# A graph transformer on one core: layer 1's attention adds its weighted values by accumulating DMAs issued from GpSimd

## The chip, the core and the metric

The kernel runs on one core of a Trainium2 chip. The core has a matrix engine (TensorE, PE in the profile), three engines for elementwise work (VectorE, DVE; ScalarE, ACT; GpSimd, POOL), an engine that only issues transfers (SyncE, SP), an on-chip memory (SBUF) of 128 partitions, a smaller accumulation memory (PSUM), and 16 DMA engines that move data between SBUF and the device's memory. Each engine takes its instructions in order from a queue of its own and waits on semaphores for the others. DMAs that GpSimd issues sit in GpSimd's queue and then in one DMA queue (q0 in the profile); SyncE and ScalarE issue into queues of their own.

The metric is the device time of one execution in microseconds.

## What is computed

Two layers of a graph transformer on 2708 tokens of width 512, with 8 heads of 64 and a feed-forward width of 2048, all in float32. The adjacency matrix has about nine neighbours in a row, and attention is masked to them:

```python
mask = adj.astype(jnp.float32) + jnp.eye(n)
q = (h @ Wq.T + bq).reshape(n, 8, 64)      # k and v alike
scores = jnp.einsum('nhd,mhd->hnm', q, k) / 8.0
scores = jnp.where(mask[None] == 0, -1e9, scores)
attn = jax.nn.softmax(scores, axis=-1)
ctx = jnp.einsum('hnm,mhd->nhd', attn, v).reshape(n, 512)
h1 = _layer_norm(h + ctx @ Wo.T + bo, ln1_g, ln1_b)
ff = relu(h1 @ W1.T + b1) @ W2.T + b2
h2 = _layer_norm(h1 + ff, ln2_g, ln2_b)    # the next layer's h
```

## The kernel before

**Lists in place of the mask.** Early in the run the kernel makes, for each token, a list of its neighbours, and sorts the tokens by the length of the lists into 22 tiles of up to 128 tokens. `CAPS` holds the longest list of each tile, from 22 entries in tile 0 to 3 in tile 21 (which has 20 tokens). Attention of a tile is then a loop over list entries: for entry s, GpSimd gathers for each of the 128 tokens one row of 1024 numbers, the key and the value of its s-th neighbour, from `kv_d` (L1113, an indirect DMA of 512 KB).

**Chunks.** The entries of a tile are taken two at a time (`SLOTS`); such a chunk is a tile `kv` of 128 x 2 x 1024 numbers. There are 111 chunks in a layer. A chunk goes through these steps:

- `weights` (L1148): VectorE multiplies the keys by the query (L1150) and sums over each head (L1156) into `sc`.
- `weigh` (L1163): ScalarE takes exponentials (L1169, into `p`). Then the values are multiplied by them, the second entry by eight ScalarE instructions (L1176), the first by one of VectorE (L1182). The first chunk of a tile writes its products straight into the accumulator `acc` (128 x 2 x 512); every later chunk writes them over its own values in `kv`, and one VectorE instruction adds those to `acc` (L1189). There are 89 such adds in a layer.
- `sums` (L1193), after a tile's last chunk: VectorE folds the two halves of `acc` together (L1197) and takes the sum of the exponentials and its reciprocal (`su`, L1209 and L1212).
- `divided` (L1215): ScalarE scales `acc` by the reciprocals into `cx` (L1220), which is what the rest of the layer asks for.

**The order by hand.** The schedule is manual: what stands earlier in the program stands earlier in its engine's queue. `attend` (L1759) is a generator that puts down one step at a time. In step k it first takes the next chunk from `loads`, which issues the gathers of chunk k + 3, then puts down `weights` of chunk k, `weigh` of chunk k - 1, `sums` if chunk k - 2 was the last of its tile, and `divided` if chunk k - 3 was. At the end, and after the second tile, empty steps let the last chunks through. In layer 1 a chunk has one of seven places in SBUF (five of the `kv` tag and two of weights that are no longer needed), so the gathers of chunk k + 3 overwrite chunk k - 4.

**Beside the feed-forward.** The tokens go through the rest of a layer in blocks of two tiles (`blocks`, L1754). `feed_forward` (L1475) runs over 16 slices f of the hidden width: eight matmuls into `pf` (L1523), the relu on ScalarE (L1534), and the second product of an earlier slice into `a` (L1496). After each slice the main loop (L1943) calls `advance`, which puts down as many steps of attention as the entry of `PACES` for that f allows; no more than three finished `cx` are held. At f = 10 and f = 11 it calls `until` for the two tiles of the next block, which puts down steps until their `cx` exist, and then `attended` (L1434) puts down their transposes (L1293), the output projection (L620, `o`) and the first layer norm. Before the last two products of a block `turned` puts down the transposes of the normed rows, and the block ends with the second norm and an indirect store of the result (L1076, `out`). Each `norm` (L1265) asks GpSimd for one small instruction, `rd` (L1275), and VectorE then waits for it (L1281). So GpSimd's queue in layer 1 holds gathers, `rd` and stores, in program order.

Layer 0 works alike, but with fewer `kv` places, and with a feed-forward of seven products instead of eight that takes more of VectorE.

Of the kernel before, what the change touches and what calls it, by code (L numbers as in the profile page):

```python
# [13 lines left out]
ALU = mybir.AluOpType  # L14
# [5 lines left out]
DM = 512  # L20
# [16 lines left out]
CAPS = (22, 14, 13, 12, 12, 11, 11, 10, 10, 9, 9, 9, 9, 8, 8, 8, 7, 7, 7, 6, 5, 3)  # L37
# [446 lines left out]
def by_edges(ctx: ExitStack, tc: tile.TileContext, x, xT, adj, layers, out, redo):  # L484
# [9 lines left out]
    nc = tc.nc  # L494
# [3 lines left out]
    NL = len(layers)  # L498
# [149 lines left out]
    def size(g):  # L648
        return min(P, N - g * P)
# [483 lines left out]
    def chunks_of(g):  # L1133
        S = CAPS[g]
        k = (S + SLOTS - 1) // SLOTS
        cuts = [-(-S * i // k) for i in range(k + 1)]
        return [(g, a, b - a) for a, b in zip(cuts, cuts[1:])]

    class Tile:


        def __init__(self, g, q):
            self.g, self.r, self.q = g, size(g), q
            self.sc = at.tile([P, LIST, NH], F32, tag="sc", name="sc", bufs=2)
            self.p = at.tile([P, LIST, NH], F32, tag="p", name="p", bufs=2)
            self.acc = None
# [16 lines left out]
        def weigh(self, kv, s0, c):  # L1163
            r, g, p = self.r, self.g, self.p
            if s0 == 0:
                self.acc = at.tile([P, SLOTS, DM], F32, tag="acc", name="acc", bufs=2)
                self.wide = c
            for s in range(s0, s0 + c):
                nc.scalar.activation(  # L1169
                    p[:r, s, :], self.sc[:r, s, :], AF.Exp, bias=minus[:r, g, s : s + 1]  # L1170
                )
            to = self.acc[:r] if s0 == 0 else kv[:r, :, DM:]
            for i in range(1, c):
                for h in range(NH):
                    hd = slice(h * DK, (h + 1) * DK)
                    nc.scalar.activation(  # L1176
                        to[:, i, hd],
                        kv[:r, i, DM + h * DK : DM + (h + 1) * DK],
                        AF.Copy,
                        scale=p[:r, s0 + i, h : h + 1],  # L1180
                    )
            nc.vector.tensor_tensor(  # L1182
                to[:, 0, :].rearrange("p (h d) -> p h d", d=DK),
                kv[:r, 0, DM:].rearrange("p (h d) -> p h d", d=DK),
                p[:r, s0, :].unsqueeze(2).to_broadcast([r, NH, DK]),
                ALU.mult,
            )
            if s0:
                nc.vector.tensor_tensor(  # L1189
                    self.acc[:r, :c, :], self.acc[:r, :c, :], kv[:r, :c, DM:], ALU.add  # L1190
                )

        def sums(self, peak):  # L1193
            r, g, S, acc, wide = self.r, self.g, CAPS[self.g], self.acc, self.wide
            while wide > 1:
                h = wide // 2
                nc.vector.tensor_tensor(  # L1197
                    acc[:r, :h, :], acc[:r, :h, :], acc[:r, wide - h : wide, :], ALU.add
                )
                wide -= h  # L1200
            nc.vector.tensor_reduce(
                peak[:r, g : g + 1],
                self.sc[:r, :S, :].rearrange("p s h -> p (s h)"),
                AX.X,
                ALU.max,
                apply_absolute_value=True,
            )
            su = small.tile([P, NH], F32, tag="su", name="su")
            nc.vector.tensor_reduce(  # L1209
                su[:r], self.p[:r, :S, :].rearrange("p s h -> p h s"), AX.X, ALU.add  # L1210
            )
            nc.vector.reciprocal(su[:r], su[:r])  # L1212
            self.su = su
# [26 lines left out]
    def loads(n):  # L1240

        ready = []
        for g, s0, c in (chunk for g in order for chunk in chunks_of(g)):
            r = size(g)
            kv = rows_of_keys(n)
            for s in range(s0, s0 + c):
                load = gather(kv[:r, s - s0, :], kv_d[n], idx[:r, g, s : s + 1])
                for move in written[n]:
                    tc.add_manual_dep(
                        load.ins,  # L1250
                        move.ins.name,
                        mybir.DependencyInfo(
                            mybir.DependencyClass.Sync, mybir.DependencyReason.DATA
                        ),
                        reason="every row of keys is in its place",
                    )
                written[n].clear()
            ready.append(kv)
            if len(ready) > EARLY:
                yield ready.pop(0)  # L1260
        yield from ready
# [497 lines left out]
    def attend(n, got):  # L1759

        peak = small.tile([P, NT], F32, tag="peak", name="peak", bufs=1)
        nc.vector.memset(peak, 0.0)
        loaded = loads(n)
        steps = []
        for g in order:
            cuts = chunks_of(g)
            steps += [(g, s0, c, i, i + 1 == len(cuts)) for i, (_, s0, c) in enumerate(cuts)]
            if g == order[1]:
                steps += [None] * 3
        steps += [None] * 3  # L1770
        kv = next(loaded)
        yield 0.0
        q, later = asked(n, order[0]), None
        done = [None] * 3
        for k, step in enumerate(steps):
            if step:
                g, s0, c, i, last = step
                if i == 0:
                    while q is None:
                        q = asked(n, g)  # L1780
                        if q is None:
                            yield None
                    t, q = Tile(g, q), None
                if k > 0:
                    kv = next(loaded)
                t.weights(kv, s0, c)
                if q is None and g != order[-1]:
                    q, later = later or asked(n, order[order.index(g) + 1]), None
                if g == order[-3] and i == 2:
                    later = asked(n, order[-1])  # L1790
                done.append((t, kv, s0, c, last))
            else:
                done.append(None)
            t3, t2, t1 = done[-4:-1]
            if t1:
                t1[0].weigh(*t1[1:4])
            if t2 and t2[-1]:
                t2[0].sums(peak)
            if t3 and t3[-1]:
                got[t3[0].g] = t3[0].divided()  # L1800
            yield c / SLOTS if step else 0.2
        nc.vector.tensor_reduce(flags[:, 4 + n : 5 + n], peak, AX.X, ALU.max)
        nc.vector.tensor_scalar(
            flags[:, 4 + n : 5 + n], flags[:, 4 + n : 5 + n], SAFE, None, ALU.is_le
        )
# [31 lines left out]
    got = {}  # L1837
# [42 lines left out]
    for n in range(NL):  # L1880
        last = n == NL - 1
        nxt = None if last else Layer(n + 1, layers[n + 1])
        if n > 0:
            streamed = now.queries(order[10:16])
            got = {}
# [196 lines left out]
```

## Time and profile before

| | |
|---|---|
| median of 2 runs | 1828.03 us (1827.94 to 1828.11) |
| the profiled execution, span from first to last instruction | 1827.1 us |
| outside the span (1828.03 - 1827.1) | 0.9 us |
| instructions | 22528 |
| mean granted TensorE clock | 0.999 |
| moved by DMA | 393.80 MB, 216 GB/s on average |
| gathers of keys and values, L1113, both layers | 420, of 1248 ns on GpSimd each |
| adds into `acc`, L1189, both layers | 178, of 1154 ns on VectorE each |
| layer 1's first block ends and its steady part begins | about 1184 us |
| layer 1's last `cx` | 1752 us |

The profiled execution's span plus 0.9 us is the median of the timed runs, so sums made on the trace can be set against the median directly. A page of the profile gives each engine's busy time as a share of the span. In a line of a group stand the source line, the engine, the operation, what is written and read, the count, then the busy time in us and the mean of one in ns, and last the idle time of that engine just before these instructions with what ended it. Busy time of an engine that others do not wait for costs nothing; what counts is which wait ends last in each stage.

### The profile page before, as it was taken

How to read it: one execution, taken by the hardware profiler on the slowest of the kernel's cores; microseconds unless marked ns; L12 is line 12 of the kernel's file. 1: busy time of each engine (PE TensorE's matmuls, PEld its weight loads, DVE VectorE, ACT ScalarE, POOL GpSimd, SP SyncE). 2: the span in 40 equal slices, each digit the busy share in tenths (PEclk: the TensorE clock that was granted, in tenths of full speed). 3: DMA queues.
4: the chain of work that ended last, by engine and by line, in shares of the span. 5: the costliest groups of instructions: out<-in, count | busy, mean ns of one | idle time of the engine just before them, and what ended most of it. 6: DMA issues, size and time to landing. Idle time of an engine off the chain costs nothing.

```text
span 1827.1 us, 22528 instructions
## 1 busy us (share of the span) xinstructions
PE 1807.5 (99%) x6563; PEld 1162.6 (64%) x6563; DVE 1457.5 (80%) x2447; ACT 949.1 (52%) x3271; POOL 798.9 (44%) x745
## 2 busy tenths in 40 slices
PE   9999999999999999999999999999999999999998
PEld 4444456666777867778677644666666666666666
DVE  5887778988989889898895257887898888889853
ACT  5771435645556545564543213665665565567531
POOL 3334755534455544454430042353464555456302
PEclk9999999999999999999999999999999999999999
DMA  9997987757576676765652876745564664555300
GB/s 340 369 335 256 371 283 245 236 169 241 195 255 228 197 236 196 219 233 181 228 191 70 287 257 248 285 160 180 178 228 150 228 224 169 195 197 194 133 14 21
DMA packets 158061, 393.80 MB, mean 216 GB/s; under 512 B 17514, under 2 KB 60894, under 8 KB 157928
## 3 DMA queue, kind: packets, MB, share of 16 engines
q0 software_dynamic: 70608, 252.12, 40.2%
q1 hardware_dynamic: 77162, 118.55, 18.7%
q10 hardware_dynamic: 10158, 21.61, 3.1%
q8 instruction: 53, 0.87, 0.2%
q14 instruction: 80, 0.66, 0.1%
HBM read 338.78 MB, written 53.44 MB: 215 GB/s over the span
## 4 chain that ended last, share of the span: by engine, by line
PE 89%; DVE 5%; issue 2%; ACT 2%; DMA 1%; POOL 1%; POOLq 0%; SPq 0%; DVEq 0%
PE pf L1523 18%; PE a L1496 17%; PE pf L1653 9%; PE k L620 8%; PE v L620 8%; PE q L620 8%; PE o L620 8%; PE c L1643 4%; PE a L1643 3%; PE tp L1293 2%; DVE sc L1156 1%; DVE kv L1150 1%; DMA forms<-form_d 1%; PE a L1677 1%; PE a L1673 1%
## 5 line engine op out<-in xcount | busy, mean ns | idle before, releaser
L1113 POOL DMA_INDIRECT kv<-kv_d,listed x420 | 524.0, 1248 | 291.2 <-DVE acc L1189 133.9
L1523 PE MATMUL pf<-hT,w 128*128 128x256 f32 (+1 forms) x1792 | 393.2, 367 | 0.1
L1523 PEld LDWEIGHTS pf<-hT,w 128*128 128x128 f32 x1792 | 323.5, 190 | 103.1 <-issue 64.4
L1496 PE MATMUL a<-w,ft 128*128 128x512 f32 x800 | 373.1, 592 | 0.0
L1176 ACT ACTIVATE kv<-kv,p 128x64 f32<-128x64 f32 x1232 | 311.0, 335 | 5.0
L1275 POOL TENSOR_TENSOR rd<-va,mhalf 128x1 f32<-128x1 f32 (+1 forms) x88 | 80.5, 914 | 520.6 <-DVE va L1273 520.5
L1150 DVE TENSOR_TENSOR kv<-kv,q 128x1024 f32<-128x1024 f32 (+1 forms) x222 | 256.9, 1157 | 13.3 <-DMA q<-q_d,ident_i 10.9
L1156 DVE TENSOR_REDUCE sc<-kv 128x16 f32<-128x1024 f32 (+1 forms) x222 | 257.9, 1162 | 7.6
L1189 DVE TENSOR_TENSOR acc<-acc,kv 128x1024 f32<-128x1024 f32 (+2 forms) x178 | 205.4, 1154 | 37.6 <-ACT kv L1176 23.0
L1653 PE MATMUL pf<-hT,w 128*128 128x256 f32 x1024 | 233.1, 379 | 1.6 <-ACT ft L1664 1.6
L1496 PEld LDWEIGHTS a<-w,ft 128*128 128x128 f32 x800 | 150.1, 190 | 113.2 <-issue 101.3
L1653 PEld LDWEIGHTS pf<-hT,w 128*128 128x128 f32 x1024 | 193.9, 190 | 35.4 <-issue 7.9
L1534 ACT ACTIVATE ft<-pf,b 128x256 f32<-128x256 f32 (+1 forms) x208 | 95.0, 459 | 197.6 <-PE pf L1523 195.2
L1169 ACT ACTIVATE p<-sc,listed 128x8 f32<-128x8 f32 x420 | 104.0, 296 | 147.2 <-DVE sc L1156 135.7
L620 PE MATMUL o<-wo,cT 128*128 128x512 f32 x336 | 151.0, 593 | 1.0 <-ACT cT L1298 1.0
L1664 ACT ACTIVATE ft<-pf,b 128x256 f32<-128x256 f32 x96 | 44.9, 468 | 160.5 <-PE pf L1653 160.5
L1182 DVE TENSOR_TENSOR kv<-kv,p 128x512 f32<-128x512 f32 (+1 forms) x178 | 123.4, 693 | 4.5 <-ACT p L1169 4.3
L620 PEld LDWEIGHTS o<-wo,cT 128*128 128x128 f32 x336 | 63.4, 190 | 74.7 <-issue 65.5
L745 DVE MAX8 tops<-code 128x8 f32<-128x247 f32 (+2 forms) x242 | 78.6, 400 | 28.3 <-ACT code L740 28.3
L1281 DVE SCALAR_TENSOR_TENSOR h<-h,rd,ln_b 128x512 f32<-128x512 f32 (+1 forms) x88 | 65.9, 749 | 39.5 <-POOL rd L1275 39.5
L1220 ACT ACTIVATE cx<-acc,su 128x64 f32<-128x64 f32 (+1 forms) x352 | 88.2, 333 | 12.9 <-DVE su L1212 7.4
L1455 DVE TENSOR_TENSOR h<-o,xb 128x512 f32<-128x512 f32 (+1 forms) x44 | 30.3, 688 | 80.0 <-PE o L620 65.0
(232 smaller groups left out, 2323.5 us busy)
## 6 DMA issues: line engine op xcount, KB each, us to landing
aj<-in_adj SPq DMA_DIRECT2D x42, 677.0 KB, 6.3
forms<-form_d SPq DMA_DIRECT2D x168, 128.0 KB, 4.2
kv_d<-kvs ACTq DMA_DIRECT2D x21, 512.0 KB, 5.5
xg<-in_xT SPq DMA_DIRECT2D x19, 512.0 KB, 7.4
w<-in_W SPq DMA_DIRECT2D x16, 512.0 KB, 6.2
kv<-kv_d,listed POOLq DMA_INDIRECT x420, 6.3
zT_d<-zT SPq DMA_DIRECT2D x22, 256.0 KB, 5.1
xb_d<-h SPq DMA_DIRECT2D x21, 256.0 KB, 5.7
```

Of the source, the lines that this page charges most:

```text
L620: nc.tensor.matmul(o[:r], xs(c), wm[:, c, :], start=(c == 0), stop=(c == NC - 1))
L1113: return nc.gpsimd.indirect_dma_start(out=to, out_offset=None, in_=table[:, :], in_offset=bass.IndirectOffsetOnAxis(ap=s, axis=0), bounds_ ...
L1150: nc.vector.tensor_tensor(kv[:r, :c, :DM], kv[:r, :c, :DM], self.q[:r].unsqueeze(1).to_broadcast([r, c, DM]), ALU.mult,)
L1156: nc.vector.tensor_reduce(self.sc[:r, s0 : s0 + c, :], kv[:r, :c, :DM].rearrange("p s (h d) -> p s h d", d=DK), AX.X, ALU.add,)
L1169: nc.scalar.activation(p[:r, s, :], self.sc[:r, s, :], AF.Exp, bias=minus[:r, g, s : s + 1])
L1176: nc.scalar.activation(to[:, i, hd], kv[:r, i, DM + h * DK : DM + (h + 1) * DK], AF.Copy, scale=p[:r, s0 + i, h : h + 1],)
L1182: nc.vector.tensor_tensor(to[:, 0, :].rearrange("p (h d) -> p h d", d=DK), kv[:r, 0, DM:].rearrange("p (h d) -> p h d", d=DK), p[:r, s0, : ...
L1189: nc.vector.tensor_tensor(self.acc[:r, :c, :], self.acc[:r, :c, :], kv[:r, :c, DM:], ALU.add)
L1496: nc.tensor.matmul(a[:r, cols], fts[f][:, c0 : c0 + r], self.w2[f // 2][:, f % 2, cols], start=(f == 0), stop=(f == NFC - 1),)
L1523: nc.tensor.matmul(pf[:, :w], self.w1[f // 2][:, c, f % 2 * P : f % 2 * P + P], hT[:, c, :w], start=(c == 0), stop=(c == NC - 1),)
L1643: nc.tensor.matmul(to, left, right, start=start, stop=stop)
L1653: nc.tensor.matmul(pf[:, :W], self.w1[j][:, c, f % 2 * P : f % 2 * P + P], hT[:, c, :], start=(c == 0), stop=(c == NC - 1),)
```

## The change

In layer 1 only (`by_dma`), the add of a later chunk leaves VectorE. A new method `added` issues it as a DMA from GpSimd whose source is the products in `kv` and whose destination is `acc`, with the operation add. It is put down one step later than the products, after the gathers of that step. The fold leaves `sums` and becomes a method of its own, `folded`; in layer 1 it is put down one step after `sums`, and `divided` one step after the fold, so that a tile's `cx` comes four steps after its last chunk and not three. One more empty step stands after the second tile and at the end. Layer 0 keeps its order.

```diff
-        def __init__(self, g, q):
+        def __init__(self, n, g, q):
             self.g, self.r, self.q = g, size(g), q
+            self.by_dma = n == NL - 1
...
-            if s0:
+            if s0 and not self.by_dma:
                 nc.vector.tensor_tensor(
                     self.acc[:r, :c, :], self.acc[:r, :c, :], kv[:r, :c, DM:], ALU.add
                 )
 
-        def sums(self, peak):
-            r, g, S, acc, wide = self.r, self.g, CAPS[self.g], self.acc, self.wide
+        def added(self, kv, s0, c):
+            r = self.r
+            if s0 and self.by_dma:
+                nc.gpsimd.dma_start(
+                    out=self.acc[:r, :c, :], in_=kv[:r, :c, DM:], accum_op=ALU.add
+                )
+
+        def folded(self):
+            r, acc, wide = self.r, self.acc, self.wide
             while wide > 1:
                 h = wide // 2
                 nc.vector.tensor_tensor(
                     acc[:r, :h, :], acc[:r, :h, :], acc[:r, wide - h : wide, :], ALU.add
                 )
                 wide -= h
+
+        def sums(self, peak):
+            r, g, S = self.r, self.g, CAPS[self.g]
...
-                steps += [None] * 3
-        steps += [None] * 3
+                steps += [None] * (3 + (n == NL - 1))
+        late = n == NL - 1
+        steps += [None] * (3 + late)
...
-            t3, t2, t1 = done[-4:-1]
+            t1, t2, t3 = done[-2], done[-3], done[-4]
+            if late and done[-5] and done[-5][-1]:
+                got[done[-5][0].g] = done[-5][0].divided()
+            if late and t2:
+                t2[0].added(*t2[1:4])
             if t1:
                 t1[0].weigh(*t1[1:4])
             if t2 and t2[-1]:
+                if not late:
+                    t2[0].folded()
                 t2[0].sums(peak)
             if t3 and t3[-1]:
-                got[t3[0].g] = t3[0].divided()
+                if late:
+                    t3[0].folded()
+                else:
+                    got[t3[0].g] = t3[0].divided()
```

More of the change, by code (lines that the diff above doesn't have):

```diff
@@ L1773, in attend @@
         q, later = asked(n, order[0]), None
-        done = [None] * 3
+        done = [None] * (3 + late)
         for k, step in enumerate(steps):
@@ L1782, in attend @@
                             yield None
-                    t, q = Tile(g, q), None
+                    t, q = Tile(n, g, q), None
                 if k > 0:
```

## The prediction

> **What bounds the kernel now.** I read the page's totals first, then the windows of layer 1, then its waits and timeline. Totals, granted clock and chain, from the page:
>
> ```profile
> PE 1807.5 (99%) x6563; PEld 1162.6 (64%) x6563; DVE 1457.5 (80%) x2447; ACT 949.1 (52%) x3271; POOL 798.9 (44%) x745
> ...
> PEclk9999999999999999999999999999999999999999
> ...
> PE 89%; DVE 5%; issue 2%; ACT 2%; DMA 1%; POOL 1%; POOLq 0%; SPq 0%; DVEq 0%
> ```
>
> TensorE is busy 99% of the span at full granted clock, and 89% of the chain that ended last is its own work. The windows show layer 1 block by block (columns: stretch, length, then busy us and count of PE, PEld, DVE, ACT, POOL, then clock, DMA share, GB/s):
>
> ```profile
> 1184.00:1248.00 64.00, 64.00 (x226) 41.28 (x225) 53.63 (x71) 39.64 (x149) 30.88 (x25) 1.00 0.52 181
> 1248.00:1312.00 64.00, 63.29 (x224) 40.59 (x222) 53.88 (x72) 38.13 (x145) 31.86 (x26) 1.00 0.55 189
> 1312.00:1376.00 64.00, 63.66 (x224) 41.23 (x225) 55.62 (x75) 38.38 (x145) 33.38 (x28) 1.00 0.55 193
> ...
> 1764.00:1827.10 63.10, 54.24 (x290) 39.92 (x288) 20.05 (x45) 9.38 (x27) 12.32 (x32) 0.97 0.04 15
> sum 792.10, PE 781.26 PEld 489.87 DVE 615.60 ACT 414.50 POOL 334.98; mean PE 65.11 PEld 40.82 DVE 51.30 ACT 34.54 POOL 27.92
> ```
>
> Of 792.1 us PE is idle 10.8, and 8.9 of these lie after 1764, where no attention is left. VectorE is 84% to 87% busy in these blocks but does not hold PE up: the two gaps at 1248 and 1312 (0.7 and 0.3 us) are all that faster attention can win back in mid-layer. So the gain has a ceiling near 1 us, and the question is what the new adds cost.
>
> **What is removed.** The adds of layer 1 on VectorE:
>
> ```profile
> L1189 DVE TENSOR_TENSOR acc<-acc,kv 128x1024 f32<-128x1024 f32 (+2 forms) x89 | 102.6, 1153 | 12.1 <-ACT kv L1176 3.9
> ```
>
> 89 instructions of 1.153 us, 102.6 us, and up to 12.1 us of idle before them. All of it lies beside PE's work, so it is worth 1.0 us on the path (both gaps) and not 102.6. The cover is the PE row itself: PE stays full whether VectorE is 86% or 70% busy.
>
> **What is added.** 89 accumulating DMAs from GpSimd. Each reads 128 x 2 rows of 2 KB (sometimes one) and the accumulator, and writes the accumulator. Before it can issue, the weighing of its chunk and the previous add into the same accumulator must have ended; behind it in POOL's queue stand the next two gathers, the norms' `rd` and the stores of `out`. The nearest rows, from 1184 to 1695 (511 us, eight blocks): POOL's and VectorE's groups, one plain DMA that POOL issues earlier, the gathers' time to landing, and the DMA share in 40 slices with the two queues.
>
> ```profile
> L1113 POOL DMA_INDIRECT kv<-kv_d,listed x165 | 205.0, 1242 | 49.3 <-issue 36.2 <-DVE sc L1156 2.7 <-ACT ft L1534 2.4
> L1275 POOL TENSOR_TENSOR rd<-va,mhalf 128x1 f32<-128x1 f32 x32 | 29.3, 917 | 190.7 <-DVE va L1273 190.6
> L1076 POOL DMA_INDIRECT out<-h,ident_i x16 | 23.0, 1440 | 18.8 <-DVE h L1281 16.2 <-DVE va L1273 2.6
> ...
> L1189 DVE TENSOR_TENSOR acc<-acc,kv 128x1024 f32<-128x1024 f32 (+2 forms) x70 | 80.9, 1156 | 7.4 <-ACT kv L1176 0.8
> ```
>
> ```profile
> L1323 POOL DMA_DIRECT2D w<-in_W x4: 801/812/840, 192.3 to 224.8; - x4
> ```
>
> ```profile
> DMA to landing us min/median/max: 3.4/6.3/9.0
> ```
>
> ```profile
> DMA  0738706389063691618906288072890739805179
> ...
> q0 software_dynamic: 24735, 89.34, 49.5%
> q1 hardware_dynamic: 4380, 7.95, 4.2%
> ```
>
> Issue: 0.8 us, as the plain DMA. The time that the 16 engines need: queue q1 moves rows of about 2 KB, and 4.2% of 511 us x 16 over 4380 packets is 78 ns each; an add has 16 such rows per engine, so one pass is 1.25 us and, with source and accumulator both read, two passes 2.5 us. Landing: no row shows an accumulate. The bounds are the gathers of the same 512 KB, 3.4 and 9.0 us (the third fence). I take the fast end plus the second pass, 3.4 + 1.25 = about 4.7, because POOL's wait gives the two gathers ahead time to drain. From one add to the next of the same tile this makes P = 4.7 + 0.8 = 5.5 us, between 4.2 and 9.8.
>
> The Trainium skill, "Collectives: The Full Stack", section "The bandwidth ceiling: the fold count and why AG ≠ RS ≠ AR", says that an add in the DMA path costs a second source read and that reads are what limits it; by that the two passes hold. The skill's "DMA: Bandwidth & Descriptors", section "Anatomy of one DMA — SWDGE (gpsimd) path", fits such a DMA as 2.0 us plus bytes over 436 GB/s, an estimate of 3.2 us for 512 KB and P near 4; the sum below would then be 1828. The trace's median of 6.3 us says that the queue, which that fit leaves out, decides here.
>
> Does it fit? POOL in the 511 us: of 70 adds 17 open a tile (the tile rate, two per block) and wait for no add, 53 are chained. 53 x 5.5 = 292; 17 x 0.8 = 14; of 165 gathers 106 issue inside the chained waits and 59 outside at 1.24 + 0.3 = 91; `rd` and `out` 29 + 23 = 52. Sum 449 of 511. POOL keeps up until P = 6.7 us, or 7.7 if `rd` and `out` fall into the waits as well; I use 7.2. DMA engines: 0.54 x 511 = 276, plus 70 x 2.5 = 175, is 451 of 511; they keep up until an add takes 3.3 us. Cost in mid-layer: nothing, by about 60 us of cover in either; gone, it costs 53 us for each us of P beyond 7.2.
>
> Nearest place where PE would feel a late tile in mid-layer: `cx` against its transpose.
>
> ```profile
> 1370.19 2.00 ACT L1220 ACTIVATE cx<-acc,su 128x64 f32<-128x64 f32 x8
> ...
> 1379.59 0.60 PE L1293 MATMUL tp<-ident,cx 128*128 128x128 f32 x4
> ```
>
> `cx` ends 7.4 us before its use. A DMA add for a VectorE add delays it by 5.5 - 1.2 = 4.3 us: covered. The moved fold and the one-step-later division add no instruction.
>
> Two places have less cover. At the start of layer 1, tile 19:
>
> ```profile
> 1118.47 1.22 DVE L1189 TENSOR_TENSOR acc<-acc,kv 128x1024 f32<-128x1024 f32 x1 [1.55 <-ACT kv L1176]
> 1119.73 0.69 DVE L1197 TENSOR_TENSOR acc<-acc 128x512 f32<-128x512 f32 x1
> ...
> 1121.26 1.76 ACT L1220 ACTIVATE cx<-acc,su 128x64 f32<-128x64 f32 x7
> ```
>
> ```profile
> 1123.99 0.60 PE L1293 MATMUL tp<-ident,cx 128*128 128x128 f32 x4
> ```
>
> Its `cx` ends at 1123.0, 1.0 us ahead. The DMA lands at 1118.5 + 5.5 = 1124.0 where VectorE ended at 1119.7: 4.3 later, less 1.0 of cover (and about 0.5 of the fold moved ahead of the sums) = +2.8 us. At the end, tile 0, the longest chain:
>
> ```profile
> 1732.60 1.23 DVE L1189 TENSOR_TENSOR acc<-acc,kv 128x1024 f32<-128x1024 f32 x1
> 1736.93 1.22 DVE L1189 TENSOR_TENSOR acc<-acc,kv 128x1024 f32<-128x1024 f32 x1
> ...
> 1747.50 1.23 DVE L1189 TENSOR_TENSOR acc<-acc,kv 128x1024 f32<-128x1024 f32 x1
> ...
> 1750.34 2.02 ACT L1220 ACTIVATE cx<-acc,su 128x64 f32<-128x64 f32 x8 [2.90 <-DVE flags L1802]
> ...
> 1759.63 0.66 PE L1293 MATMUL tp<-ident,cx 128*128 128x128 f32 x4
> ```
>
> Its last five adds run from 1732.6 to 1748.7. As a chain they end at 1732.6 + 5 x 5.5 = 1760.1; fold 0.7 and `cx` 2.0 make 1762.8, 3.2 us after PE wants it.
>
> **The sum.** Against the span of 1827.1: -1.0 (gaps) + 2.8 (start) + 3.2 (end) + 0 (mid-layer) = +5.0. Outside the span lie 0.9 us, to the median of 1828.03: 1833.0 us. With P from 4.2 to 7.2 the same sum runs from 1828 to 1845 (start 1.5 to 4.5, end 0 to 11.7, gaps 0 to -1), the likeliest case's own range.
>
> **Rivals.** (1) POOL's chain becomes the bound (slower). Place: the add of chunk k-2 waits in POOL for the add of k-3, with the gathers and `rd` queued behind. For it: VectorE waits for `rd` as it is,
>
> ```profile
> L1281 DVE SCALAR_TENSOR_TENSOR h<-h,rd,ln_b 128x512 f32<-128x512 f32 x32 | 24.0, 751 | 15.7 <-POOL rd L1275 15.7
> ```
>
> and the 6.3 us median landing would make P 7.1, only just inside. Against: that median comes from bursts in which gathers follow each other every 1.5 us. Halfway to the slowest landing P is 8.5: 53 x 1.3 = 69 us in mid-layer, start 5.8, end 18.2, less 1.0: 1920. By the same terms it decides (over 2%, 36.6 us) from P = 7.6.
>
> (2) The DMA engines fill up (slower). If an accumulated row takes twice the two passes, an add costs 5.0 us: 276 + 350 = 626 for 511, +115, with start and end 1949. It decides from about 3.7 us per add. Against: nothing in the trace; for it: their share is already 0.52 to 0.55, and the line of 40 slices above shows it at 8 or 9 tenths after each pause.
>
> (3) Everything is hidden, start and end too: 1827. For it: VectorE, 1.2 us lighter per chunk, reaches the last weighing earlier than I let it; against: 1.0 us of cover at the start.
>
> (4) Faster by 2%: it would need 36.6 us where PE leaves 10.8. Excluded but for a slip in reading.
>
> **How the numbers follow.** Forecast 0.50, rival 1 0.22, rival 2 0.10, rival 3 0.17, rival 4 0.01. About 2% is what a measurement of this kernel can tell from no change: faster 0.01, same 0.50 + 0.17 = 0.67, slower 0.32. The range goes from 1826 (just under rival 3) to 1920 (rival 1's price); left out are rival 2 and the dearer part of rival 1, some 0.17.
>
> **What would show it.** Right: L1189 gone in layer 1, VectorE's share about 15 points lower in mid-layer, POOL's wait for its own add near 4.7 us, PE still 63 to 64 us in each 64 us block, small PE gaps before the first and last `cx` transposes. Wrong: `rd` waits on VectorE growing from half a us to several, PE gaps in every block (rival 1), DMA share near 0.95 in mid-layer (rival 2), or no gap near 1124 and 1760 (rival 3). An add that lands in over 7 us breaks the forecast.

## The result, and the profile after

The changed kernel takes 1955.29 us (1955.07 to 1955.51, two runs) against 1828.03 (1827.94 to 1828.11): 1.0685 times as long, 95% interval 1.0639 to 1.0731. It is slower by 127 us, where 1833 was forecast with 1920 as the upper bound.

From the page of the changed kernel come the totals, the granted clock and the DMA share in 40 slices, GpSimd's DMA queue, the shares of the chain that ended last, and the costliest groups:

```profile
PE 1839.9 (94%) x6563; PEld 1175.9 (60%) x6563; DVE 1358.2 (70%) x2358; ACT 945.0 (48%) x3271; POOL 902.3 (46%) x834
...
PEclk9999999999999999999999999988989999998999
DMA  9988986666766757747446977877698898887610
...
q0 software_dynamic: 93184, 295.42, 50.7%
...
PE 55%; DMA 19%; DVE 10%; issue 8%; POOL 4%; ACT 3%; POOLq 0%; DVEq 0%; ACTq 0%
...
L1197 POOL DMA_DIRECT2D acc<-kv x89 | 113.7, 1277 | 193.2 <-DMA acc<-kv 69.0
...
L1231 ACT ACTIVATE cx<-acc,su 128x64 f32<-128x64 f32 (+1 forms) x352 | 88.5, 334 | 174.0 <-DVE acc L1205 160.0
...
L1205 DVE TENSOR_TENSOR acc<-acc 128x512 f32<-128x512 f32 (+1 forms) x44 | 30.2, 686 | 151.8 <-DMA acc<-kv 151.8
...
L1292 DVE SCALAR_TENSOR_TENSOR h<-h,rd,ln_b 128x512 f32<-128x512 f32 (+1 forms) x88 | 66.0, 749 | 95.0 <-POOL rd L1286 95.0
...
acc<-kv POOLq DMA_DIRECT2D x77, 512.0 KB, 6.1
```

VectorE is relieved as written: 1358.2 us where it was 1457.5. Yet the span is 1953.8 where it was 1827.1, 126.7 more. TensorE's busy time rose by 32.4 us (1839.9 - 1807.5) for the same 6563 matmuls, and its idle time by 94.3 (from 19.6 to 113.9). The two make the 126.7. Of the chain that ended last TensorE now has 55%, not 89%, and DMA 19%, not 1%. New is the wait of the fold (L1205), 151.8 us, and right behind it the one of the division (L1231), 160.0 us of waiting for that fold.

A mark that both kernels pass once in each block is the transposes of the normed rows (`tp<-ident,h`). In the first block and in the tenth of eleven they stand here in the kernel before (L1293) and in the changed one (L1304):

```profile
1138.17 1.04 PE L1293 MATMUL tp<-ident,h 128*128 128x128 f32 x8
...
1715.80 1.04 PE L1293 MATMUL tp<-ident,h 128*128 128x128 f32 x8
```

```profile
1148.31 1.04 PE L1304 MATMUL tp<-ident,h 128*128 128x128 f32 x8
...
1826.31 1.04 PE L1304 MATMUL tp<-ident,h 128*128 128x128 f32 x8
```

The changed kernel is 10.1 us late at the first mark, 110.5 at the second and 126.7 at its end. So the start costs 10.1 us, the nine blocks between the marks 100.4, and the end 16.2.

The windows (columns as in the prediction) show the loss from the start of layer 1's attention on:

```profile
1100.00:1184.00 84.00, 77.97 (x228) 40.96 (x227) 48.37 (x71) 35.49 (x139) 30.82 (x28) 0.96 0.82 255
1184.00:1248.00 64.00, 58.94 (x195) 37.00 (x194) 40.91 (x60) 32.42 (x123) 32.10 (x27) 0.95 0.75 208
1248.00:1312.00 64.00, 48.81 (x156) 28.65 (x155) 33.51 (x46) 31.67 (x121) 30.55 (x27) 0.87 0.79 218
1312.00:1376.00 64.00, 51.77 (x176) 33.26 (x175) 34.14 (x49) 28.52 (x108) 33.58 (x29) 0.89 0.82 225
...
1631.00:1695.00 64.00, 58.44 (x194) 36.48 (x193) 37.02 (x52) 33.19 (x128) 35.87 (x31) 0.95 0.90 237
```

The waits of the same kernel from 1035 us on (engine and line, for whom; us in total, times, the longest):

```profile
ACT cx L1231 <- DVE acc L1205: 160.0, 17, 16.6
DVE acc L1205 <- DMA acc<-kv: 151.8, 20, 17.0
...
DVE h L1292 <- POOL rd L1286: 77.6, 46, 10.0
...
PE pf L1534 <- ACT ft L1545: 48.3, 9, 12.5
...
PE o L620 <- ACT cT L1309: 28.6, 4, 15.2
...
PE tp L1304 <- ACT cx L1231: 8.1, 3, 4.7
```

TensorE itself waits mostly for ScalarE's relus (`ft`) and its copies of transposed rows (`cT`), 76.9 us, and only 8.1 us for a `cx`.

No engine is full in the 64 us stretches shown: TensorE 49 to 59 us of 64, VectorE 34 to 41 where it was 54 to 57, GpSimd 31 to 36, the DMA engines at 0.75 to 0.90. The engines stand and wait for each other. One tile (tile 10) shows how, in the timeline of the changed kernel (start, length, instruction; in brackets the idle time before it; only the rows that the text below uses):

```profile
1328.13 1.38 POOL L1197 DMA_DIRECT2D acc<-kv  x1
1330.16 0.68 DVE L1183 TENSOR_TENSOR kv<-kv,p 128x512 f32<-128x512 f32 x1
1336.29 1.32 POOL L1197 DMA_DIRECT2D acc<-kv  x1 [4.13 <-ACT p L1170]
1338.20 0.81 ACT L1545 ACTIVATE ft<-pf,b 128x256 f32<-128x256 f32 x2
1341.62 0.68 DVE L1183 TENSOR_TENSOR kv<-kv,p 128x512 f32<-128x512 f32 x1
1342.19 1.30 POOL L1197 DMA_DIRECT2D acc<-kv  x1 [0.87 <-DVE sc L1157]
1345.04 0.60 PE L1304 MATMUL tp<-ident,cx 128*128 128x128 f32 x4
1347.21 1.88 PE L1507 MATMUL a<-w,ft 128*128 128x512 f32 x4
1348.61 0.95 POOL L1197 DMA_DIRECT2D acc<-kv  x1 [2.48 <-DMA acc<-kv]
1352.68 0.69 DVE L1205 TENSOR_TENSOR acc<-acc 128x512 f32<-128x512 f32 x1 [10.37 <-DMA acc<-kv]
1352.92 1.32 POOL L1113 DMA_INDIRECT kv<-kv_d,listed  x1 [2.01 <-DMA acc<-kv]
1353.41 2.02 ACT L1231 ACTIVATE cx<-acc,su 128x64 f32<-128x64 f32 x8 [14.40 <-DVE acc L1205]
1355.54 1.34 POOL L1197 DMA_DIRECT2D acc<-kv  x1
...
1360.91 1.11 ACT L1309 ACTIVATE cT<-tp,bv 128x128 f32<-128x128 f32 x4
1361.32 6.07 PE L620 MATMUL o<-wo,cT 128*128 128x512 f32 x8 [12.23 <-ACT cT L1309]
1367.22 0.60 PE L1304 MATMUL tp<-ident,cx 128*128 128x128 f32 x4
```

This tile has four chained adds. They start 8.2, 5.9 and 6.4 us apart, the last lands 4.1 us after its start, and together they take 24.6 us (1328.13 to 1352.68). The tile's last products were ready at 1330.84, and its fold starts 21.8 us after that. VectorE finds two chunks of the next tile to do, then it stands 10.4 us at the fold. ScalarE stands 14.4 us at the division (`cx`) behind it, and here the wait becomes dear: behind `cx` in ScalarE's queue are relus of the feed-forward (`ft`, none between 1339.0 and 1357.8) and the copies of the block's first tile (`cT`), which has nothing to do with this sum. Its transposes were done at 1345.6, but `cT` starts only at 1360.91. TensorE ends its products at 1349.09 and has nothing for 12.2 us. The late tile's own `cx` ends at 1355.43 and is not asked for until 1367.22 (its transposes), 11.8 us later. It was not late for its reader; it stood in the way of others.

About the same time in the kernel before, last products and fold of another tile of nine entries (tile 11):

```profile
1363.91 0.68 DVE L1182 TENSOR_TENSOR kv<-kv,p 128x512 f32<-128x512 f32 x1
...
1368.26 0.68 DVE L1197 TENSOR_TENSOR acc<-acc 128x512 f32<-128x512 f32 x1
```

There the fold comes 3.7 us after the products are ready (1368.26 - 1364.59), with no wait; tile 10 itself has the same 3.7 us there. The change, its later place of the fold included, made it 18.2 us later against that.

The row of 1361.32 holds the other part of the loss. Eight matmuls of the output projection took 6.07 us after that wait; eight such matmuls behind no wait, earlier in the same trace:

```profile
1292.39 3.60 PE L620 MATMUL o<-wo,cT 128*128 128x512 f32 x8
```

The granted clock falls to 0.87 in the worst block and is 0.974 over the run (0.999 before). The Trainium skill, "TensorE: Matmul & The Clock Gate", section "What's actually happening", says that after an idle window of about 3.4 us the array runs at half clock until about 3.4 us of work have passed. The trace agrees in kind: each long gap is paid for a second time by slow matmuls. After each of the twelve pauses of 2.9 us and more in layer 1 the next 16 matmuls took 1.9 to 3.8 us longer than such matmuls do in the median of the kernel before, 31.1 us together, which is nearly all of the 32.4 us, a quarter of the loss.

### The profile page after: what moved, and what is told of

Same layout as the page of the kernel before. It is cut to its first block, busy times and chain, and to the rows that moved or that the text cites. A ratio compares the mean times of both kernels' runs of the same rounds, so it can differ in the third digit from the quotient of the medians.

```text
span 1953.8 us, 22552 instructions
## 1 busy us (share of the span) xinstructions
PE 1839.9 (94%) x6563; PEld 1175.9 (60%) x6563; DVE 1358.2 (70%) x2358; ACT 945.0 (48%) x3271; POOL 902.3 (46%) x834
## 3 DMA queue, kind: packets, MB, share of 16 engines
q0 software_dynamic: 93184, 295.42, 50.7%
## 4 chain that ended last, share of the span: by engine, by line
PE 55%; DMA 19%; DVE 10%; issue 8%; POOL 4%; ACT 3%; POOLq 0%; DVEq 0%; ACTq 0%
DMA acc<-kv 16%; PE pf L1664 9%; PE k L620 7%; PE v L620 7%; PE q L620 6%; PE o L620 5%; PE pf L1534 4%; PE c L1654 4%; PE a L1507 4%; PE a L1654 3%; DVE kv L1151 2%; DVE sc L1157 2%; DMA kv<-kv_d,listed 2%; POOL kv L1113 2%; PE tp L1304 2%
## 5 line engine op out<-in xcount | busy, mean ns | idle before, releaser
L1113 POOL DMA_INDIRECT kv<-kv_d,listed x420 | 517.0, 1231 | 294.6 <-DVE acc L1190 125.8
L1534 PE MATMUL pf<-hT,w 128*128 128x256 f32 (+1 forms) x1792 | 408.8, 377 | 48.8 <-ACT ft L1545 48.7
L1534 PEld LDWEIGHTS pf<-hT,w 128*128 128x128 f32 x1792 | 332.2, 195 | 159.0 <-issue 62.5
L1507 PE MATMUL a<-w,ft 128*128 128x512 f32 x800 | 377.8, 597 | 7.0 <-ACT ft L1545 3.8
L1664 PEld LDWEIGHTS pf<-hT,w 128*128 128x128 f32 x1024 | 193.9, 190 | 35.4 <-issue 7.9
L1197 POOL DMA_DIRECT2D acc<-kv x89 | 113.7, 1277 | 193.2 <-DMA acc<-kv 69.0
L620 PE MATMUL o<-wo,cT 128*128 128x512 f32 x336 | 159.1, 619 | 28.6 <-ACT cT L1309 28.6
L1231 ACT ACTIVATE cx<-acc,su 128x64 f32<-128x64 f32 (+1 forms) x352 | 88.5, 334 | 174.0 <-DVE acc L1205 160.0
L1205 DVE TENSOR_TENSOR acc<-acc 128x512 f32<-128x512 f32 (+1 forms) x44 | 30.2, 686 | 151.8 <-DMA acc<-kv 151.8
L1183 DVE TENSOR_TENSOR kv<-kv,p 128x512 f32<-128x512 f32 (+1 forms) x178 | 123.2, 693 | 16.3 <-ACT p L1170 16.2
L1190 DVE TENSOR_TENSOR acc<-acc,kv 128x1024 f32<-128x1024 f32 (+2 forms) x89 | 102.8, 1155 | 25.5 <-ACT kv L1177 19.1
```

Of the source, the lines that this page charges most:

```text
L620: nc.tensor.matmul(o[:r], xs(c), wm[:, c, :], start=(c == 0), stop=(c == NC - 1))
L1113: return nc.gpsimd.indirect_dma_start(out=to, out_offset=None, in_=table[:, :], in_offset=bass.IndirectOffsetOnAxis(ap=s, axis=0), bounds_ ...
L1183: nc.vector.tensor_tensor(to[:, 0, :].rearrange("p (h d) -> p h d", d=DK), kv[:r, 0, DM:].rearrange("p (h d) -> p h d", d=DK), p[:r, s0, : ...
L1197: nc.gpsimd.dma_start(out=self.acc[:r, :c, :], in_=kv[:r, :c, DM:], accum_op=ALU.add)
L1507: nc.tensor.matmul(a[:r, cols], fts[f][:, c0 : c0 + r], self.w2[f // 2][:, f % 2, cols], start=(f == 0), stop=(f == NFC - 1),)
L1534: nc.tensor.matmul(pf[:, :w], self.w1[f // 2][:, c, f % 2 * P : f % 2 * P + P], hT[:, c, :w], start=(c == 0), stop=(c == NC - 1),)
```

## The experiments

The first theory was the one that the timeline suggests: the chain of adds ends too late for a fold that stands in order on VectorE, `cx` waits for it on ScalarE, and what TensorE needs stands behind `cx`. The rivals were the load on the DMA engines, the price of the accumulating DMA itself, the changed order, and GpSimd's queue, in which adds stand behind gathers and `rd` behind both. Times are of single runs unless an interval is given, each with the kernel before run on the same chip in brackets; that one gave 1827.95 to 1832.24, so a few us between groups mean nothing. Edits are against the changed kernel unless said otherwise.

**Order alone.** The add goes back to VectorE, at the new place and in the new order.

```diff
-                nc.gpsimd.dma_start(
-                    out=self.acc[:r, :c, :], in_=kv[:r, :c, DM:], accum_op=ALU.add
-                )
+                nc.vector.tensor_tensor(
+                    self.acc[:r, :c, :], self.acc[:r, :c, :], kv[:r, :c, DM:], ALU.add
+                )
```

> The changed order (adds one step later, fold and division each put down later), but with the 89 adds on VectorE at the place where the DMA stood. Chain theory (the adds follow each other at the DMA's latency, and VectorE and ScalarE stand in order at the fold and the division): the order alone costs nothing, 1826 to 1832 us. So say the load theory (DMA engines too full) and the queue theory (GpSimd's queue, with gathers and rd behind the adds). Rival, the order itself: the division one step later misses TensorE's transposes, above 1850 us.

1830.68 us [1832.24]. The later add, fold and division cost nothing.

**No adds at all.** The DMA is replaced by `pass`, so a tile's sum holds its first chunk alone.

> The changed order with the adds of layer 1 left out altogether (the output is then not the sum over all neighbours). All theories: 1826 to 1828 us, since TensorE had about 1 us of gaps to give back in layer 1; this is the ceiling of what relief of VectorE can be worth. If VectorE was holding TensorE up in a way the busy times hide, below 1820 us.

1833.28 us [1832.24]. VectorE has 102 us less to do and nothing comes of it: TensorE is busy 580 of 580 us between 1184 and 1764, and was for 579 before. The gain had no room, as predicted.

**Load alone.** The kernel before, with its adds on VectorE, also issues an accumulating DMA of the same size per later chunk, from the eighth tile on, into a spare buffer that nobody reads (67 of them).

```diff
+        def added(self, kv, s0, c):
+            r = self.r
+            if s0:
+                to = spares()
+                nc.gpsimd.dma_start(out=to[:r, :c, :], in_=kv[:r, :c, DM:], accum_op=ALU.add)
...
+            if n == NL - 1 and t2 and order.index(t2[0].g) >= FREE:
+                t2[0].added(*t2[1:4])
```

> The kernel before, adds on VectorE, and beside them 67 accumulating DMAs of the same shape (from the eighth tile of layer 1 on) into two spare places that nobody reads, issued from GpSimd one step after the products; the gather that takes the chunk's place waits for them, the fold does not. Chain theory: the load and GpSimd's queue cost little, 1828 to 1840 us. Load or queue theory: about three quarters of the 127 us, 1900 to 1925 us, with DMA share 0.75 to 0.85 after 1310 us.

1844.70 us [1832.24]: 12.5 more. Windows of this kernel (same columns), the first two stretches with such DMAs:

```profile
1310.00:1437.00 127.00, 120.43 (x414) 76.18 (x413) 105.97 (x142) 71.33 (x267) 80.62 (x67) 0.99 0.89 244
1437.00:1565.00 128.00, 125.26 (x438) 79.92 (x437) 107.73 (x141) 78.29 (x297) 82.69 (x71) 1.00 0.92 260
```

The DMA share is 0.89 to 0.92, above nearly all blocks of the changed kernel, and GpSimd issues the same kind of instructions, 67 adds for 89; TensorE still works 120 and 125 us. Nearly full DMA engines cost a tenth of the loss when nobody waits for the sums (only a gather that takes a chunk's place waits for its DMA).

**The price of one add.** The same DMAs without the operation, so that each copy overwrites the sum.

```diff
-                    out=self.acc[:r, :c, :], in_=kv[:r, :c, DM:], accum_op=ALU.add
+                    out=self.acc[:r, :c, :], in_=kv[:r, :c, DM:]
```

> The same 89 DMAs with the same waits, but as plain copies without the add (so the sums are left out). One pass over the rows for two. Chain theory: the landing gets shorter by about one pass, 1.3 us of the 6.1, so a period of about 6.1 in place of 7.4 us and some 60 to 90 us less: 1865 to 1900 us, with the same kind of wait at the fold. Load theory: the added DMA share falls from 0.26 to 0.13 in mid-layer and with it half of the loss: 1885 to 1895 us, with no wait left at the fold that a late gather does not explain.

1879.78 us [1832.24]: 47.5 of the 127 are left. From its page and its waits (line numbers two lower):

```profile
q0 software_dynamic: 82608, 295.42, 45.9%
```

```profile
DVE acc L1203 <- DMA acc<-kv: 102.5, 20, 9.2
```

A cheaper DMA makes the same wait shorter, not away: still 20 waits, of 5.1 us instead of 7.6. The wait, and not the addition, is the kind of cost. Its length is the price of the DMA, and that weighs much: with about half of the DMA engines' time per transfer some 80 us of the loss are gone. The lower load is a part of this that the run does not split off; the whole load of 67 adds cost 12.5 us above.

**Moving the fold.** Fold and division one more step later (`done[-5]` folded, `done[-6]` divided, one more empty step at both places).

```diff
-        late = n == NL - 1
+        late = 2 * (n == NL - 1)
...
-            if late and done[-5] and done[-5][-1]:
-                got[done[-5][0].g] = done[-5][0].divided()
+            if late and done[-6] and done[-6][-1]:
+                got[done[-6][0].g] = done[-6][0].divided()
...
+            if late and done[-5] and done[-5][-1]:
+                done[-5][0].folded()
```

> The changed kernel, with fold and division each put down one step later again (two steps behind the place they had on VectorE, one empty step more at the ends and after tile 21). Chain theory: what costs is that VectorE and ScalarE stand at the fold and the division, in order; one step is 5 to 6 us, so the fold's wait of 152 us falls below 80 and the time to 1870 to 1910 us. If the chain is too slow as such (a period above what a step gives), the wait moves to the gathers and little is won: above 1930 us.

1928.28 us [1831.95], 27 less than the changed kernel; more was expected. Waits of this kernel:

```profile
DVE h L1292 <- POOL rd L1286: 116.9, 46, 12.1
...
DVE acc L1205 <- DMA acc<-kv: 82.5, 14, 16.7
```

The fold's wait halves and the wait for `rd` grows from 77.6 to 116.9 us: what VectorE does not lose at the fold it loses at the norms, whose `rd` stands in GpSimd's queue behind adds that wait.

**Two chains.** From the eighth tile on, every other add goes to a second accumulator, which VectorE adds before the fold; a chain has half the length. The second chunk's products are written straight into that accumulator, so 74 of the 89 DMAs are left.

```diff
-            if s0 and self.by_dma:
+            if s0 > SLOTS * self.pair and self.by_dma:
+                acc = self.acc2 if self.pair and s0 // SLOTS % 2 else self.acc
                 nc.gpsimd.dma_start(
-                    out=self.acc[:r, :c, :], in_=kv[:r, :c, DM:], accum_op=ALU.add
+                    out=acc[:r, :c, :], in_=kv[:r, :c, DM:], accum_op=ALU.add
```

> From the eighth tile of layer 1 on, a tile has two accumulators that its chunks fill in turn (the second stands in the place of wq, free by then; VectorE adds the two at the fold, 1.2 us a tile), so an add waits for the one before the last and no longer for the last. Chain theory: GpSimd's waits for its own adds go from there, the fold waits for one landing and no more, and the blocks after 1310 us get shorter by 3 to 5 us each: 1890 to 1925 us. Queue theory (only GpSimd's queue and issue time count): no change, 1945 to 1960 us.

1928.89 us [1831.95]: 26 less, a little short of the expected. Halving the chain alone does not mend it.

**`rd` off GpSimd.** In layer 1's norms VectorE copies the variance in place of GpSimd's inverse root.

```diff
-        nc.gpsimd.tensor_tensor(rd[:r], va[:r], mhalf[:r], ALU.pow)
+        if last:
+            nc.vector.tensor_copy(rd[:r], va[:r])
+        else:
+            nc.gpsimd.tensor_tensor(rd[:r], va[:r], mhalf[:r], ALU.pow)
```

> The changed kernel, with rd of layer 1's norms on VectorE and off GpSimd (the variance itself stands in for its inverse root there, so layer 1's norms are not the reference's). Queue theory: the 78 us that VectorE waited for rd behind adds and gathers come back, 1875 to 1900 us. Chain theory: those waits lie beside the wait at the fold, 1935 to 1955 us.

1919.42 us [1831.95]: 36 less, between the two expectations; the fold still waits 139.5 us. Both waits count, and neither is the whole.

**Both moved, and all three.** The later fold with `rd` on VectorE, and these two with the second accumulator.

> Fold and division one step later and rd off GpSimd, both together (layer 1's norms use the variance itself). Alone they won 27 and 36 us on 1955. If the two waits lie one behind the other in VectorE's order, they add: 1885 to 1900 us. If one hides the other: 1910 to 1920 us.

1884.83 us [1827.95]: 70 less than the changed kernel, near the 27 + 36 of the two alone. These two waits add up.

> Two accumulators from the eighth tile on, fold and division one step later, rd off GpSimd (layer 1's norms use the variance itself). Chain theory: with these no add waits for the last one, the fold has a landing's time, and rd waits for nobody; what is left is the start and the load: 1845 to 1875 us. If DMA load or GpSimd's issue time is a cause of its own beside the chain, it stays above 1880 us.

1870.99 us [1827.95]. 43 us are left.

**The last adds on VectorE.** First only the last add of each tile, then the last two (three where the count of its entries is odd), put down on VectorE just before the fold.

```diff
+            if s0 + c >= CAPS[self.g] - 2 * SLOTS + 1:
+                self.kept = getattr(self, "kept", []) + [(kv, c)]
+                for kv, c in self.kept if last else ():
+                    nc.vector.tensor_tensor(
+                        self.acc[:r, :c, :], self.acc[:r, :c, :], kv[:r, :c, DM:], ALU.add
+                    )
+            else:
                 nc.gpsimd.dma_start(
```

The kernel with only the last one has `>= CAPS[self.g]` in the first line.

> The changed kernel, but only the last add of each tile done by VectorE (one step before the fold); 67 DMAs stay. Chain theory: what VectorE meets is then the landing of the add before the last, one step earlier, so about one period of 7 us less per tile: the fold's 152 us fall to 30 to 70 and the time to 1855 to 1890 us. Load or queue theory: 67 of 89 DMAs keep three quarters of the loss, 1915 to 1925 us.

1936.54 us [1827.95], far above what the chain theory expected and somewhat above the rival's range too. Its waits:

```profile
DVE acc L1201 <- DMA acc<-kv: 133.7, 16, 12.6
```

The wait only moved from the fold to VectorE's own add (L1201), which stands one step ahead of the fold and needs the DMA before it: that one is late as well.

> The changed kernel, but the last two adds of each tile done by VectorE, just before the fold; the DMAs (about half of the 89) are the earlier ones, with two steps until VectorE touches the accumulator. Chain theory: no wait at the fold for want of time, 1828 to 1845 us. Load theory: half of the loss stays, 1885 to 1895 us.

1842.36 us [1831.95], as expected. 36 adds stay DMAs, VectorE's 53 adds wait 9.6 us in all, and 10 us of loss are left. With two adds of slack a chain is out of the way of the fold. Fewer DMAs have a share in this too: this run cannot split slack from count.

**The add ahead of the gathers.** Within a step, the add is put down before the two gathers and not behind them.

```diff
+            if late and done[-2]:
+                done[-2][0].added(*done[-2][1:4])
...
-            if late and t2:
-                t2[0].added(*t2[1:4])
```

> The changed kernel, with each add put down ahead of the two gathers of its step and not behind them. Chain theory: an add issues up to 2.6 us earlier and finds less in the DMA queue, so the period falls from 7.4 towards 6 us: 1915 to 1940 us. If the gathers were the late ones, they get later by an add and nothing is won: 1950 to 1975 us.

1902.26 us [1827.95]: 53 less, the most that one edit alone won, and more than expected. The fold's wait falls to 79.0 us. Where the add stands in GpSimd's queue was worth more here than halving the chain.

**The add first, and the fold later; and two chains besides.**

> Adds ahead of the gathers, and fold and division one step later. Alone they won 53 and 27 us on 1955. If place in the queue and time to the fold are two shares of one lateness, together they win most of their sum: 1870 to 1890 us. If the place alone was the cause, the later fold adds nothing: 1895 to 1905 us.

1896.70 us [1829.43]: only 5.6 less than the add first alone, in the range that was expected if the place alone was the cause. The later fold, worth 27 us by itself, is worth next to nothing behind the other edit. Its waits:

```profile
DVE h L1292 <- POOL rd L1286: 91.6, 46, 9.3
...
DVE acc L1205 <- DMA acc<-kv: 27.2, 2, 14.3
```

The fold hardly waits for a DMA any more, `rd` does, and the tile itself is still late: ScalarE's `cx` still stands 57.1 us for the fold.

> The same with two accumulators from the eighth tile on, so that no add waits for the last one. If the chain still costs once the place is mended, 10 to 25 us below first_later, 1850 to 1875 us; if not, the same as first_later or slightly above for the 15 more adds on VectorE.

1865.77 us [1829.43], 31 below the run before it: the length of the chain counts once the queue is mended. Its windows, of which the second accumulator acts from the third on:

```profile
1035.00:1184.00 149.00, 140.42 (x442) 70.83 (x441) 78.91 (x117) 48.04 (x180) 52.18 (x46) 0.97 0.79 262
1184.00:1310.00 126.00, 115.42 (x388) 72.41 (x387) 84.95 (x123) 67.69 (x254) 72.27 (x62) 0.96 0.88 249
1310.00:1437.00 127.00, 124.78 (x435) 79.17 (x434) 91.87 (x127) 73.94 (x279) 79.25 (x64) 1.00 0.81 234
1437.00:1565.00 128.00, 124.94 (x437) 79.90 (x436) 96.28 (x129) 80.59 (x309) 84.53 (x69) 1.00 0.85 257
1565.00:1692.00 127.00, 127.00 (x448) 82.07 (x447) 94.74 (x132) 78.97 (x297) 80.21 (x64) 1.00 0.81 234
...
1770.00:1870.00 100.00, 83.18 (x398) 58.01 (x396) 27.68 (x60) 19.29 (x61) 14.38 (x34) 0.95 0.10 23
```

This is the clearest view of the cause. Once chains are halved, adds stand ahead of gathers and the fold is a step later, TensorE is idle 5.3 us in the 382 from 1310 to 1692, with 74 of the 89 accumulating DMAs still in place and the DMA share at 0.81 to 0.85. What is left of the loss is mostly before 1310, where there is one accumulator (19.2 us idle), and in slow matmuls after those gaps (clock 0.96 to 0.97). The end, from 1770 to the span's end at 1864.0, has 10.8 us idle, hardly more than the 8.9 of the kernel before.

**The add first, the last two on VectorE.** The best of these edits, timed against the kernel before.

> Adds ahead of the gathers, and the last two or three adds of each tile on VectorE just before the fold (36 DMAs). Chain theory: every DMA has landed by then, TensorE has no gap, 1827 to 1834 us on a chip where the kernel before takes 1828; nothing can be won beyond that, since TensorE is full. If GpSimd's added 48 us of issue or the load cost by themselves, 1838 to 1845 us as with early_adds.

1832.03 us (1830.26 to 1833.56) against 1829.43 (1826.93 to 1831.78): 1.0013 times, 95% interval 1.0003 to 1.0023. TensorE is full in each stretch from 1184 to 1770, with 36 of the 89 adds as DMAs. It does not beat the kernel before; with TensorE at 99% there was nothing to win.

**What this settles.** The order has no part in the loss, and the load about a tenth (12.5 us for 67 of the 89 DMAs). The loss is lateness: a tile's sum is ready only after a chain of DMAs, each issued from a queue in which gathers stand ahead of it, while VectorE and ScalarE, in fixed order, stand before that sum with other work behind it. Chain, place in the queue, place of the fold and `rd` each carry 26 to 53 us when mended alone. The fold and `rd` add up (27, 36, and 70 together), the fold and the place in the queue overlap (27, 53, and 59 together), so the split of the 127 us between them stays open. No run moved the division alone: that TensorE suffers through ScalarE's queue rests on the timeline and on the waits of the changed kernel.

## Why the prediction was wrong

- *What bounds the kernel; the ceiling of 1 us.* Right: leaving the adds out won nothing.
- *Issue 0.8 us, from a plain DMA.* Too low: 1.277 us (the group of L1197). The nearest row was of another kind of DMA.
- *Two passes, 2.5 us of the DMA engines per add.* Nearly right. GpSimd's queue's share times the span rose from 0.402 x 1827.1 = 734.5 to 0.507 x 1953.8 = 990.6 us; over 89 adds that is 2.88 us each. The plain copies took (0.459 x 1878.1 - 734.5) / 89 = 1.43 us. An add took twice the time of a copy (2.88 / 1.43). This agrees with the second source read that the prediction takes from the Trainium skill, "Collectives: The Full Stack", section "The bandwidth ceiling: the fold count and why AG ≠ RS ≠ AR".
- *Landing 4.7 us, P = 5.5.* Too low. From issue to landing an add of 512 KB took 6.1 us in the median, and of the 53 adds whose landing the trace gives 18 took over 7 us, the sign named for breaking the forecast. From the start of one add (L1197) to that of the next of the same tile it was 8.3 us in the mean over the 51 such pairs from 1184 to 1770 (median 8.0), and 7.4 over the 39 of them before which GpSimd stood idle. The tile shown, with 6.8 in the mean, is a quick one. So P passed the 7.2 us from which the prediction let it cost anything. By the prediction's own terms (start P - 2.7, end 5P - 24.3, mid-layer 53 for each us beyond 7.2) P = 7.4 gives 1855 us and P = 8.3 gives 1908. The size of P is one part of the miss, 27 to 80 us of the 127, and part of these 8.3 us is itself waiting for other engines.
- *"Does it fit? ... Cost in mid-layer: nothing, by about 60 us of cover".* This is the step that failed: the blocks between the two marks above cost 100.4 us. Beside the low P, the form of the sum is wrong. It adds up GpSimd's time over eight blocks, its waits for landings included, as if the chains could slide past the other engines. In the tile shown they cannot. VectorE may not pass the fold and stands 10.4 us. GpSimd's gather at 1352.92 waits 2.0 us for the place that the last add still reads, and the first add of the next tile stands behind it: its products were ready at 1342.30, it starts at 1355.54. So one late landing held VectorE, ScalarE and the next chain at once. The run with the later fold shows that this has a price of its own: its adds were as far apart (8.2 us in the mean of 53 pairs), and moving the fold alone still won 27 us, for which the sum has no term.
- *"A DMA add for a VectorE add delays it by 5.5 - 1.2 = 4.3 us: covered."* Wrong twice. It counts one add: in the tile shown one add was in flight and three not issued when the last products were ready, and the fold came 18.2 us later. The prediction had set the end of layer 1 out as a chain of five and did not do the same for other tiles. And it asks only whether `cx` is in time for its own transposes. It still was, by 11.8 us. What it did not name is what is queued behind the waiting `cx` on ScalarE: relus and another tile's `cT`. TensorE waits 76.9 us for relus and `cT` in all, and 8.1 for a `cx`.
- *VectorE as pure relief.* Not counted was that a VectorE without adds may reach the fold sooner and so leave the chain less time; this is argued, no run isolates it.
- *Start and end, +2.8 and +3.2.* Both too low: 10.1 us at the first mark and 16.2 behind the second. At tile 19 the wait was nearly as forecast (TensorE stands 3.3 us until 1129.1 for its `cx`); the rest are smaller gaps (6.0 us idle in all from 1100 to 1184) and slow matmuls. At the end tile 0's last five adds take 30.6 us to the fold (1840.89 to 1871.53) where VectorE's took 16.2, so 14.5 more, with 11.4 forecast; slow matmuls come on top.
- *Rivals.* Rival 1 is the one that came. Its signs are there: `rd` waits on VectorE went from 22.1 us to 77.6 over 46 times, nine of them above 2 us, and there are gaps in every block. The P of 7.6 from which it was to decide was passed by the mean of 8.3, but its price was too low: 1908 at that P by its terms, against 1955.3 measured, for it came from the same sum. Rival 2 (DMA engines full) did not happen: 0.75 to 0.90 in the blocks shown, and 0.92 was bearable. Rivals 3 and 4 are out. The clock that falls after each gap was in no term; the slow matmuls are 32.4 us.

## What to carry to other kernels

Before moving dependent steps to a slower path, write out the chain for one tile from its last input to its first reader, and ask of every engine that will stand waiting what is queued behind; a sum of busy time over many blocks says nothing about waits that stand in order on several engines. An accumulating DMA was cheap here for sums that nobody waits for soon, so give it the first adds of a group, keep the last ones on the engine that reads the sum, and put it ahead of bulk transfers in its queue. If TensorE is full, relieving another engine wins nothing to set against that risk.

## What the runs showed of the hardware

- An accumulating copy of mostly 512 KB between places in SBUF took 2.88 us of the 16 DMA engines against 1.43 us for a plain one, with 254 packets instead of 135 ((93184 - 70608) / 89 and (82608 - 70608) / 89), while the bytes that the profile counts are the same (295.42 MB).
- GpSimd spent 1.28 us on the issue of an accumulating DMA and 0.74 us on that of a plain one of the same shapes (means; the latter in the run with plain copies).
- Accumulating DMAs into the same place followed each other in 8.3 us in the mean of 51 pairs, 5.7 at the quickest, beside gathers; VectorE's add of the same data took 1.15 us.
- Eight matmuls took 6.07 us after a pause of 12.2 us and 3.60 us without; over the kernel TensorE's matmuls took 32.4 us longer, a part of the 126.7.
- A DMA share of 0.92 over 128 us, unread sums among it, left TensorE 98% busy (125.26 of 128).
